# Row-by-row fetches in five steps instead of eight, and two transfers moved to ScalarE's queue, in a graph attention layer

## The chip, the cores and the metric

The kernel runs on one core of a Trainium2 chip. Five engines work in parallel, each in its own fixed order: TensorE (PE, with its weight loads as PEld), VectorE (DVE), ScalarE (ACT), GpSimd (POOL) and SyncE (SP). SyncE, ScalarE and GpSimd can issue transfers, which 16 shared DMA engines carry out. The metric is the device time of one execution in microseconds, as the median over runs; lower is better.

## The reference

One layer of relational graph attention over 3125 nodes with 128 features, 100,000 edges sorted by destination, 5 edge types and 8 heads of 16. Cut to what matters:

```python
for r in range(5):
    q = x[dst] @ W_Q[r];  k = x[src] @ W_K[r];  v = x[src] @ W_V[r]      # per edge, 8 heads
    logits = (q * k).sum(-1) / 4 + attn_bias[r]                          # only edges of type r
    attn = exp(logits - segment_max(logits, dst)) / segment_sum(exp(...), dst)
    out += segment_sum(attn * v, dst)
out = out @ out_proj_w.T + out_proj_b
x = layernorm(x + layernorm(out + x) * ln_gamma + ln_beta)
```

## The kernel before

**Tables first.** A prologue (25 blocks of 128 nodes) computes for each node and each of the 5 types the key and value row (256 numbers of 4 bytes, 1 KB) and writes them to a table `kv_d` in memory; the queries go to `q_d`. From the lists of sources, destinations and types it also makes the row numbers `idx` for gathering, the keys `key_d` (which row of a window of queries an edge needs) and the masks `msk_d` (where a new destination begins).

**Then a loop over edges.** The edges are cut into tiles of 128, four tiles to a group of 512, and three groups to a step: 66 steps (`NST`), the first and the last with two groups. The rows of a tile come into a ring of four places (`place(k)`: three in `kv_early`, one in `kv_late`). In step `k` VectorE multiplies the gathered keys with the queries (`products`, L975), sums them by head (`logits`, L1033) and sets them apart by type (`closed_lanes`); TensorE turns them; two scans of VectorE (L1115, L1119) find the running maximum, which need the masks `mk`; ScalarE takes the exponentials (`exps`, L1137); TensorE turns them back; VectorE weighs the values (`weigh`, L1160), and TensorE sums them by destination (`sums`, L1194) against a matrix that ScalarE makes (`places`, L1173, L1177). Two steps later the sums are divided (`norm`) and put in place (`by_node`), and blocks of nodes that are complete go through the output projection and the two norms.

**Where a tile's rows come from.** Three ways:
- GpSimd gathers most tiles from `kv_d`, one indirect transfer a tile (L849). `point(k, j, leave)` says, at eleven points of a step, up to which tile GpSimd has gathered by then, and after which instruction (`leave`).
- The first tile of each step from 3 to 65 isn't gathered from the table: GpSimd gathers its rows of `x` in the prologue (`xg`, L377), and in the loop ScalarE and TensorE make keys and values of them (`early_places`, `early_turn`, `early_rows`); ScalarE copies them to their place (`early_keep`, L1109).
- In every eighth step (`PERIOD`) one tile is fetched by SyncE, row by row: `own_fetch(k)` loads 16 row numbers into registers (L869) and issues 16 transfers of 1 KB (L875) in each of eight steps; then ScalarE copies the tile to its place (`own_copy`, L883).

**What else is fetched.** `take(k, leave)` runs once a step behind the products and issues on SyncE: the masks of step `k + 2` (`fetch_masks`, L936), the keys of step `k + 3` (`fetch_keys`, L719), and three windows of query rows for step `k + 3` (`fetch_rows`, L743, with a load of three numbers, L704). `own_fetch(k)` follows in the same queue.

**Where the ring's places join.** A step's products cover the tiles from its second one to the first one of the next step, and that one lies at the start of the next place. Between places in `kv_early` that is one stretch. In two of four steps it is two pieces of memory, and `runs` makes two instructions of each product and each sum.

Of the kernel before, what the change touches and what calls it, by code (L numbers as in the profile page):

```python
# [9 lines left out]
F32 = mybir.dt.float32  # L10
BF16 = mybir.dt.bfloat16
# [8 lines left out]
P = 128  # L20
# [3 lines left out]
R = 5  # L24
# [32 lines left out]
WINB = 3 * H * 2  # L57
NTILE = -(-E // P)
LANES = R * HEADS
L3 = G3 * LANES  # L60
SEG = 64
QWB = 10
# [87 lines left out]
def windowed_path(  # L150
# [20 lines left out]
    q_d = dram.tile([NP * R * 3, H], BF16, name="q_d")  # L171
    key_d = dram.tile([NGR, GE], BF16, name="key_d")
    msk_d = dram.tile([NGR, MW], BF16, name="msk_d")


    def keep(name, shape, dt=F32):
        return const.tile(shape, dt, name=name)
# [7 lines left out]
    rows_at = keep("rows_at", [HG, 2, P], I32)  # L185
    oT = keep("oT", [P, N + WN])
    out_wT = keep("out_wT", [P, H])
    gamma_t = keep("gamma_t", [P, H])
# [7 lines left out]

    def kv_tile(name, n):
        pool = ctx.enter_context(tc.tile_pool(name=f"pool_{name}", bufs=1))
        return pool.tile([P, n * T * G3, KVW], F32, name=name)

    early = kv_tile("kv_early", KVA)

# [356 lines left out]
        nc.scalar.copy(typr, typ_r)  # L559

    def own_rows():
        nc.vector.tensor_scalar_mul(rows_at, kvrow[:, :, P : 2 * P], float(KVW * 4))

    msk = load.tile([HG, 2, MW], BF16, name="msk")

# [97 lines left out]
    def late_x():  # L663
# [48 lines left out]

    SPE, ACTE = mybir.EngineType.SP, mybir.EngineType.Activation

    def fetch_keys(k, leave=None):
# [3 lines left out]
        behind(nc.sync.dma_start(kt[:, : n * P], keys.partition_broadcast(P)), leave)  # L719

    def spot(k):
        n = (B0[k + 1] - B0[k]) * P
# [11 lines left out]
        live["hot", k] = hot  # L734
        return made

    def fetch_rows(k, leave=None):
        a, b = G0[k] + (k > 0), min(G0[k + 1] + 1, NGR)
        bytes_ = q_d.rearrange("n h -> (n h)").bitcast(U8)
        for g, f in zip(range(a, b), starts(window, a, b, SPE)):  # L740
            live["qw", g] = qw = ahead.tile([P, 3, H], BF16, name="qw", bufs=QWB)
            behind(
                nc.sync.dma_start(  # L743
                    qw.rearrange("p s h -> p (s h)").bitcast(U8),
                    bytes_[bass.ds(f, P * WINB)].rearrange("(p h) -> p h", h=WINB),
                ),
                leave,
            )

    made = {}  # L750

# [43 lines left out]
    along(keyr, 0, put_key)  # L795
    along(keyr, 1, put_key)
    begins()
    spills()
    types(1, range(R))()
    project_weights()  # L800
# [16 lines left out]
    def place(k):  # L817
        at = k % KVB
        return (early, at * T * G3) if at < KVA else (late, (at - KVA) * T * G3)

    def runs(a, b):
        out_ = []
        for q in range(a, b):
            k = AT[q // T][0]
            kv, at = place(k)
# [31 lines left out]
            issued.append(q)  # L857

    def own_fetch(k):
        at = (k - 2) // PERIOD * PERIOD + PERIOD + 3  # L860
        if at not in OWN_AT:
            return
        i = (k - 2) % PERIOD * ROWS
        if i == 0:
            live["own", at] = flow.tile([P, KVW], F32, name="own")
        n = min(ROWS, P - i)
        g = OWN_AT[at] // T
        bytes_ = kv_d.rearrange("n h -> (n h)").bitcast(U8)
        _, rows = nc.values_load_multi_w_load_instructions(  # L869
            rows_at[g % HG : g % HG + 1, g // HG, i : i + n], engines=[SPE], min_val=0,  # L870
            max_val=(N * R - 1) * KVW * 4,
            skip_runtime_bounds_check_because="sources are nodes, types are relations",
        )
        for p, f in enumerate(rows, i):
            nc.sync.dma_start(  # L875
                live["own", at][p : p + 1].bitcast(U8).rearrange("o (a b) -> o a b", a=2),
                bytes_[bass.ds(f, KVW * 4)].rearrange("(o a b) -> o a b", o=1, a=2),
            )
# [49 lines left out]
        live.pop(("xT", b))  # L928
        store_rows(b, live.pop(("q3", b)))

    def fetch_masks(k, leave=None):
        n = len(groups(k))
        live["mk", k] = mk = flow.tile([L3, MW], BF16, name="mk", bufs=3)
        rows = msk_d[G0[k] : G0[k] + n]
        behind(
            nc.sync.dma_start(  # L936
                mk[: n * LANES, :],
                bass.AP(tensor=rows.tensor, offset=rows.offset, ap=[[MW, n], [0, LANES], [1, MW]]),
            ),
            leave,  # L940
        )

    def spread_q(k):
# [161 lines left out]
            )  # L1105

    def early_keep(k):
        ((kv, c0, _),) = runs(B0[k + 1] - 1, B0[k + 1])
        nc.scalar.copy(kv[:, c0, :], live.pop("rows"))  # L1109

    def scans(k):
        n = len(groups(k)) * LANES
# [293 lines left out]
    spot(1)  # L1406
    fetch_keys(2)
    fetch_rows(2)

    def take(k, leave):  # L1410
# [12 lines left out]
    for k in range(NST - 1):  # L1423
        new, old = k >= 1, k >= 2
        q0, (q, c0, c1), (q1, d0, _) = q_at.get(k), half(k), half(k - 1)
        done, rooted = block_at.get(k), block_at.get(k - 1)
        place_g, sum_g = list(groups(k - 1)), list(groups(k - 1))

        def place_next():
            return places(place_g.pop(0)) if place_g else None  # L1430

        def sum_next():
            if sum_g:
                sums(sum_g.pop(0))
# [681 lines left out]
```

## Time and profile before

| | us |
|---|---|
| median of 3 runs (1009.69 to 1012.93) | 1010.77 |
| the profiled execution, as timed | 1009.02 |
| its span from the first to the last instruction | 1007.2 |
| busy: PE 926.2, DVE 899.2, POOL 741.2, ACT 716.3 | |
| mean granted TensorE clock | 0.979 |

A busy time counts what an engine executes; for SyncE nothing is counted, since issuing a transfer is no busy time, and its timeline is read instead (marked SPq). A row of the timeline gives the start, the length, engine and line, and in brackets the idle time before it with what ended that. A row of a group gives the count, then for one line the shortest, median and longest duration in ns, or busy time and mean ns, and then the idle time before. A row of waits gives the total, the count and the longest. For a transfer the row's length is that of its issue, not of the moving of data.

### The profile page before, as it was taken

How to read it: one execution, taken by the hardware profiler on the slowest of the kernel's cores; microseconds unless marked ns; L12 is line 12 of the kernel's file. 1: busy time of each engine (PE TensorE's matmuls, PEld its weight loads, DVE VectorE, ACT ScalarE, POOL GpSimd, SP SyncE). 2: the span in 40 equal slices, each digit the busy share in tenths (PEclk: the TensorE clock that was granted, in tenths of full speed). 3: DMA queues.
4: the chain of work that ended last, by engine and by line, in shares of the span. 5: the costliest groups of instructions: out<-in, count | busy, mean ns of one | idle time of the engine just before them, and what ended most of it. 6: DMA issues, size and time to landing. Idle time of an engine off the chain costs nothing.

```text
span 1007.2 us, 23071 instructions
## 1 busy us (share of the span) xinstructions
PE 926.2 (92%) x6983; PEld 717.2 (71%) x6983; DVE 899.2 (89%) x1517; ACT 716.3 (71%) x1956; POOL 741.2 (74%) x793
## 2 busy tenths in 40 slices
PE   7995689999999999999999999999999999999986
PEld 3553577777777777777777777778777777777774
DVE  3666788999999999999999999999999999899997
ACT  2443377777787787778777777778777777777765
POOL 7777777777777777777777777777777777777760
PEclk9996799999999999999999999999999999999998
DMA  8997766567666666666666667665666765666630
GB/s 210 356 355 252 206 159 194 158 198 194 177 194 182 179 175 194 177 195 195 177 167 193 195 177 194 178 191 171 193 177 193 194 191 161 185 195 176 160 100 11
DMA packets 100547, 189.60 MB, mean 188 GB/s; under 512 B 19901, under 2 KB 61201, under 8 KB 100298
## 3 DMA queue, kind: packets, MB, share of 16 engines
q0 software_dynamic: 36192, 97.50, 34.9%
q1 hardware_dynamic: 63032, 89.66, 29.7%
q10 hardware_dynamic: 1194, 0.92, 0.4%
q8 instruction: 56, 0.92, 0.4%
q14 instruction: 73, 0.60, 0.2%
HBM read 157.61 MB, written 30.40 MB: 187 GB/s over the span
## 4 chain that ended last, share of the span: by engine, by line
DVE 39%; PE 24%; DMA 21%; issue 8%; POOL 4%; ACT 3%; DVEq 0%; POOLq 0%; ACTq 0%
DMA kv_early<-kv_d,idx 16%; DVE qe L1033 7%; DVE kv_early L975 6%; PE both L1194 5%; PE pr L514 4%; DVE wv L1160 4%; DVE run L1115 4%; DVE run L1119 3%; POOL kv_early L849 3%; PE qe L953 3%; DVE kv_late L975 2%; PE mid L1102 2%; DVE lx L1008 2%; DMA kv_late<-kv_d,idx 2%; PE lt L1092 2%
## 5 line engine op out<-in xcount | busy, mean ns | idle before, releaser
L849 POOL DMA_INDIRECT kv_early<-kv_d,idx x543 | 515.4, 949 | 166.6 <-issue 85.1
L1194 PE MATMUL both<-wv,at 128*125 128x136 f32 x1528 | 261.6, 296 | 0.0
L1173 ACT ACTIVATE at<-wide_at,nkey 128x125 f32<-128x125 f32 x776 | 245.0, 388 | 0.0
L1194 PEld LDWEIGHTS both<-wv,at 128*125 128x125 f32 x1528 | 201.8, 187 | 49.9 <-issue 44.4
L849 POOL DMA_INDIRECT kv_late<-kv_d,idx x169 | 160.0, 947 | 51.5 <-issue 27.1
L1102 PE MATMUL mid<-wkv,xr 128*128 128x256 f32 x630 | 146.5, 379 | 1.6 <-ACT xr L1096 1.6
L953 PE MATMUL qe<-qw,hot 128*128 128x128 bf16 x2349 | 146.1, 222 | 0.0
L953 PEld LDWEIGHTS <-hot 128*128 128x128 bf16 x2352 | 141.6, 102 | 0.5 <-DVE vio L650 0.4
L1102 PEld LDWEIGHTS mid<-wkv,xr 128*128 128x128 f32 x630 | 115.0, 190 | 15.0 <-ACT xr L1096 1.9
L1177 ACT ACTIVATE at<-at 128x500 f32<-128x500 f32 x194 | 120.3, 620 | 6.1
L975 DVE TENSOR_TENSOR kv_early<-kv_early,qe 128x1536 f32<-128x1536 f32 (+3 forms) x70 | 89.3, 1277 | 27.2 <-DMA kv_early<-kv_d,idx 22.0
L1115 DVE TENSOR_TENSOR_SCAN run<-mk,lt 120x640 f32<-120x640 bf16 (+1 forms) x66 | 97.6, 1478 | 1.5 <-PE lt L1065 1.5
L1259 ACT COPY oT<-fin 128x25 f32 x188 | 33.9, 180 | 81.9 <-PE fin L1255 77.9
L1119 DVE TENSOR_TENSOR_SCAN run<-lt,run 120x576 f32<-120x576 bf16 (+1 forms) x65 | 88.2, 1357 | 2.2
L1033 DVE TENSOR_REDUCE qe<-kv_early 128x96 f32<-128x1536 f32 (+2 forms) x65 | 86.7, 1334 | 2.2
L1160 DVE TENSOR_TENSOR wv<-kv_early,mid 128x1536 f32<-128x1536 f32 (+2 forms) x51 | 86.1, 1691 | 1.8 <-PE mid L1102 1.5
L1092 PE MATMUL lt<-diag,xg 128*128 128x512 f32 x252 | 83.5, 454 | 0.0
L1065 PE MATMUL lt<-ident,lx 128*120 128x128 f32 (+2 forms) x396 | 54.7, 275 | 24.6 <-DVE lx L1008 8.6
L1065 PEld LDWEIGHTS lt<-ident,lx 128*120 128x120 f32 (+2 forms) x396 | 38.5, 136 | 52.7 <-ACT diag L1086 20.2
L1144 PEld LDWEIGHTS mid<-gather_heads,ls 120*128 120x128 f32 (+1 forms) x528 | 64.2, 191 | 16.1 <-ACT xTq L901 12.1
L1144 PE MATMUL mid<-gather_heads,ls 120*128 120x24 f32 (+1 forms) x528 | 67.0, 265 | 9.4 <-ACT xTq L901 7.2
L1189 PE MATMUL both<-wv,over 128*5 128x136 f32 x380 | 75.3, 280 | 0.0
(232 smaller groups left out, 1341.5 us busy)
## 6 DMA issues: line engine op xcount, KB each, us to landing
kt<-key_d SPq DMA_DIRECT2D x64, 384.0 KB
qw<-q_d SPq DMA_DIRECT2D x196, 96.0 KB
kv_d<-kvs SPq DMA_DIRECT2D x24, 640.0 KB
own<-kv_d SPq DMA_DIRECT2D x896, 1.0 KB
q_d<-q SPq DMA_DIRECT2D x25, 480.0 KB
mk<-msk_d SPq DMA_DIRECT2D x64, 150.5 KB
kv_early<-kv_d,idx POOLq DMA_INDIRECT x543
kv_late<-kv_d,idx POOLq DMA_INDIRECT x169
```

The costliest lines, as they stand in the source:

```text
L849: nc.gpsimd.indirect_dma_start(out=kv[:, at, :], out_offset=None, in_=kv_d[:, :], in_offset=bass.IndirectOffsetOnAxis(ap=idx[:, q % T, q / ...
L953: spread = nc.tensor.matmul(dest[j], hot[:, j * P : (j + 1) * P], qw[:, c, :], start=(c == 0), stop=(c == 2),)
L975: made = nc.vector.tensor_tensor(kv[:, c0:c1, :H], kv[:, c0:c1, :H], qe[:, n:m], op=ALU.mult)
L1033: made = nc.vector.tensor_reduce(lg[:, n : n + c1 - c0], heads(kv[:, c0:c1, :H]), AX.X, ALU.add)
L1102: nc.tensor.matmul(rows, xr[:, r * P : (r + 1) * P], wkv[:, r].rearrange("h s c -> h (s c)"), start=(r == 0), stop=(r == R - 1),)
L1115: there = nc.vector.tensor_tensor_scan(run[:n], mk[:n, 1 : WIDE + 1], lt, -BIG, op0=ALU.add, op1=ALU.max)
L1119: back = nc.vector.tensor_tensor_scan(run[:n, SEG:][:, ::-1], masks[:, SEG:][:, ::-1], run[:n, SEG:][:, ::-1], -BIG, op0=ALU.add, op1=ALU.max,
L1144: nc.tensor.matmul(ex.rearrange("p (i t) k -> p t i k", t=T)[:, t], ls[: n * LANES, t * P : (t + 1) * P], gather_heads[: n * LANES, :n], s ...
L1160: return nc.vector.tensor_tensor(heads(wv[:, a:b, :H]), heads(kv[:, at + a : at + b, H:]), ex[:, a:b, :, None].to_broadcast([P, b - a, HEA ...
L1173: nc.scalar.activation(at[:, t, :], row_at[:, :WR], AF.Abs, bias=nkey[:, t, g : g + 1], scale=1.0)
L1177: return nc.scalar.activation(at[:, :n], at[:, :n], AF.Relu, bias=1.0, scale=-1.0)
L1194: nc.tensor.matmul(pp[:WR], at[:, t, :], wv[:, T * i + t, :], start=(t == 0), stop=(t == end))
```

## The change

- `PERIOD` becomes 5: 12 tiles instead of 7 are fetched row by row, 26 rows a step instead of 16. Their row numbers go to memory in the prologue (`row_d`) and from there, together with the windows' row numbers, into a table with one row for each step (`at_step`). One load (`load_step`) then fetches both kinds, four steps ahead, in the middle of the rows of the step.
- Masks and keys are issued by ScalarE, behind the second scan and ahead of the exponentials (`ahead_of_both`), and no longer wait for the products. `take` keeps the query rows alone.
- In step 1 the masks from step 6 on are copied five times over in memory (`many_d`); from step 6 a step's masks are read from 15 rows, 8 times each, instead of 3 rows, 40 times each.
- Each place of the ring gets one column more. The first tile of the next step lies there or at the start of the next place, whichever follows without a break; for that `early_keep` copies its keys and its values apart where the places don't join. Products and sums are then one instruction in these steps.

```diff
-PERIOD = 8
+PERIOD = 5
+COPIES = 5
+COPIED = 6
...
-        return pool.tile([P, n * T * G3, KVW], F32, name=name)
+        return pool.tile([P, n * T * G3 + 1, KVW], F32, name=name)
...
-        11: [keys_b],
-        12: [sorted_rows],
-        13: [masks_a],
+        11: [keys_b, own_steps(0)],
+        12: [sorted_rows, own_steps(1)],
+        13: [masks_a, own_steps(2), own_steps(3)],
...
+    def load_step(k):
+        if not 3 <= k < NST - 1:
+            return
+        own = own_part(k - 3)
+        n = own[2] if own else 0
+        _, at = nc.values_load_multi_w_load_instructions(
+            at_step[k : k + 1, : G3 + n], engines=[SPE], min_val=0,
...
+    def beyond(k):
+        kv, at = place(k)
+        return kv, at + T * G3
...
-            at += q - T * G0[k]
+            if q == T * G0[k] and k - 1 in early_at:
+                kv, at = beyond(k - 1)
+            else:
+                kv, at = place(k)
+                at += q - T * G0[k]
...
         for p, f in enumerate(rows, i):
+            if p == i + n // 2:
+                load_step(k + 4)
             nc.sync.dma_start(
...
-    def fetch_masks(k, leave=None):
+    def fetch_masks(k, queue=nc.sync):
...
+        c = COPIES if k >= COPIED else 1
+        rows = (many_d if c > 1 else msk_d)[G0[k] : G0[k] + n]
+        queue.dma_start(
+            mk[: n * LANES, :],
+            bass.AP(
+                tensor=rows.tensor, offset=rows.offset,
+                ap=[[MW, n * c], [0, LANES // c], [1, MW]],
             ),
...
     def early_keep(k):
-        ((kv, c0, _),) = runs(B0[k + 1] - 1, B0[k + 1])
-        nc.scalar.copy(kv[:, c0, :], live.pop("rows"))
+        rows, (kv, c0), (to, c1) = live.pop("rows"), beyond(k), place(k + 1)
+        if kv is to and c0 == c1:
+            nc.scalar.copy(kv[:, c0, :], rows)
+        else:
+            nc.scalar.copy(kv[:, c0, :H], rows[:, :H])
+            nc.scalar.copy(to[:, c1, H:], rows[:, H:])
...
     def take(k, leave):
+        if k + 3 < NST:
+            fetch_rows(k + 3, leave)
+
+    def ahead_of_both(k):
         if k + 2 < NST:
-            fetch_masks(k + 2, leave)
+            fetch_masks(k + 2, nc.scalar)
         if k + 3 < NST:
-            fetch_keys(k + 3, leave)
-            fetch_rows(k + 3, leave)
+            fetch_keys(k + 3, nc.scalar)
...
             take(k, made)
-            if k >= 2:
-                own_fetch(k)
+            own_fetch(k)
+            if k == 1:
+                copy_masks()
...
         for j, leave in enumerate(scans(k)):
             point(k, 2 + j, leave)
+        ahead_of_both(k)
```

More of the change, by code (lines that the diff above doesn't have):

```diff
@@ L173, in windowed_path @@
     msk_d = dram.tile([NGR, MW], BF16, name="msk_d")
+    many_d = dram.tile([NGR, COPIES, MW], BF16, name="many_d")
+    row_d = dram.tile([HG * 2 * P + P], I32, name="row_d")
     def keep(name, shape, dt=F32):
@@ L184, in windowed_path @@
     window = keep("window", [1, NGR], I32)
-    rows_at = keep("rows_at", [HG, 2, P], I32)
+    at_step = keep("at_step", [NST, G3 + ROWS], I32)
     oT = keep("oT", [P, N + WN])
@@ L561, in own_rows, with own_steps, run, window_steps @@
     def own_rows():
-        nc.vector.tensor_scalar_mul(rows_at, kvrow[:, :, P : 2 * P], float(KVW * 4))
+        rows_at = srt.rearrange("g s i -> g (s i)").bitcast(I32)[:, : 2 * P]
+        nc.vector.tensor_scalar_mul(
+            rows_at.rearrange("g (s i) -> g s i", s=2), kvrow[:, :, P : 2 * P], float(KVW * 4)
+        )
+        nc.sync.dma_start(
+            row_d[: HG * 2 * P].rearrange("(g i) -> g i", g=HG), rows_at
+        )
+    def own_steps(i):
+        def run():
+            for k in list(OWN_AT)[i::4]:
+                g = OWN_AT[k] // T
+                a, f = (g % HG * 2 + g // HG) * P, k - PERIOD - 1 + 3
+                nc.sync.dma_start(
+                    at_step[f : f + PERIOD, G3:],
+                    row_d[a : a + PERIOD * ROWS].rearrange("(i j) -> i j", j=ROWS),
+                )
+        return run
+    def window_steps():
+        nc.sync.dma_start(
+            at_step[3 : NST - 1, :G3],
+            window[:, G0[3] + 1 : G0[NST - 1] + 1].rearrange("o (k j) -> o k j", j=G3),
+        )
     msk = load.tile([HG, 2, MW], BF16, name="msk")
@@ L713, in windowed_path, with fetch_keys @@
     SPE, ACTE = mybir.EngineType.SP, mybir.EngineType.Activation
-    def fetch_keys(k, leave=None):
+    def fetch_keys(k, queue=nc.sync):
         n = B0[k + 1] - B0[k]
@@ L718, in fetch_keys @@
         keys = key_d.rearrange("g e -> (g e)")[B0[k] * P : B0[k + 1] * P]
-        behind(nc.sync.dma_start(kt[:, : n * P], keys.partition_broadcast(P)), leave)
+        queue.dma_start(kt[:, : n * P], keys.partition_broadcast(P))
     def spot(k):
@@ L735, in spot @@
         return made
+    def load_step(k):
[5 more added lines that the diff above has]
+            at_step[k : k + 1, : G3 + n], engines=[SPE], min_val=0,
+            max_val=(N * R - 1) * KVW * 4,
+            skip_runtime_bounds_check_because="rows of nodes, sources and types",
+        )
+        live["at_step", k] = [
+            nc.s_assert_within(
+                f, 0, (N - 1) * R * WINB,
+                skip_runtime_bounds_check_because="destinations are nodes",
+            )
+            for f in at[:G3]
+        ] + list(at[G3:])
     def fetch_rows(k, leave=None):
@@ L739, in fetch_rows @@
         bytes_ = q_d.rearrange("n h -> (n h)").bitcast(U8)
-        for g, f in zip(range(a, b), starts(window, a, b, SPE)):
+        if 3 <= k < NST - 1:
+            at = live.pop(("at_step", k))
+            live["rows_at", k - 3] = at[G3:]
+        else:
+            at = starts(window, a, b, SPE)
+        for g, f in zip(range(a, b), at):
             live["qw", g] = qw = ahead.tile([P, 3, H], BF16, name="qw", bufs=QWB)
@@ L748, in fetch_rows, with own_part @@
             )
+    def own_part(k):
+        at = (k - 2) // PERIOD * PERIOD + PERIOD + 3
+        if k < 2 or at not in OWN_AT:
+            return None
+        i = (k - 2) % PERIOD * ROWS
+        return at, i, min(ROWS, P - i)
     made = {}
@@ L797, in windowed_path @@
     begins()
+    window_steps()
     spills()
@@ L824, in runs @@
             k = AT[q // T][0]
-            kv, at = place(k)
-            at += q - T * G0[k]
+            if q == T * G0[k] and k - 1 in early_at:
[3 more added lines that the diff above has]
+                at += q - T * G0[k]
             if out_ and out_[-1][0] is kv and out_[-1][2] == at:
@@ L859, in own_fetch @@
     def own_fetch(k):
-        at = (k - 2) // PERIOD * PERIOD + PERIOD + 3
-        if at not in OWN_AT:
+        rows = live.pop(("rows_at", k), None)
+        if not rows:
+            load_step(k + 4)
             return
-        i = (k - 2) % PERIOD * ROWS
+        at, i, n = own_part(k)
         if i == 0:
             live["own", at] = flow.tile([P, KVW], F32, name="own")
-        n = min(ROWS, P - i)
-        g = OWN_AT[at] // T
         bytes_ = kv_d.rearrange("n h -> (n h)").bitcast(U8)
[L869 to L873, printed above, removed]
         for p, f in enumerate(rows, i):
+            if p == i + n // 2:
+                load_step(k + 4)
             nc.sync.dma_start(
@@ L929, in store_q, with copy_masks @@
         store_rows(b, live.pop(("q3", b)))
-    def fetch_masks(k, leave=None):
+    def fetch_masks(k, queue=nc.sync):
         n = len(groups(k))
         live["mk", k] = mk = flow.tile([L3, MW], BF16, name="mk", bufs=3)
[L934 to L938, printed above, removed]
-            ),
-            leave,
+        c = COPIES if k >= COPIED else 1
[5 more added lines that the diff above has]
+                ap=[[MW, n * c], [0, LANES // c], [1, MW]],
+            ),
+        )
+    def copy_masks():
+        nc.sync.dma_start(
+            many_d[G0[COPIED] :],
+            msk_d[G0[COPIED] :, None, :].to_broadcast([NGR - G0[COPIED], COPIES, MW]),
         )
@@ L1107, in early_keep @@
     def early_keep(k):
-        ((kv, c0, _),) = runs(B0[k + 1] - 1, B0[k + 1])
-        nc.scalar.copy(kv[:, c0, :], live.pop("rows"))
+        rows, (kv, c0), (to, c1) = live.pop("rows"), beyond(k), place(k + 1)
+        if kv is to and c0 == c1:
+            nc.scalar.copy(kv[:, c0, :], rows)
+        else:
+            nc.scalar.copy(kv[:, c0, :H], rows[:, :H])
+            nc.scalar.copy(to[:, c1, H:], rows[:, H:])
     def scans(k):
@@ L1408, in windowed_path @@
     fetch_rows(2)
+    load_step(3)
     def take(k, leave):
+        if k + 3 < NST:
+            fetch_rows(k + 3, leave)
+    def ahead_of_both(k):
         if k + 2 < NST:
-            fetch_masks(k + 2, leave)
+            fetch_masks(k + 2, nc.scalar)
         if k + 3 < NST:
-            fetch_keys(k + 3, leave)
-            fetch_rows(k + 3, leave)
+            fetch_keys(k + 3, nc.scalar)
     def half(k):
```

## The prediction

> **What bounds the kernel now.** I read the busy shares first, then the stretches, then each engine's waits, and only then the chain. In one stretch of 600 us from the middle (columns: length, then PE, PEld, DVE, ACT and POOL busy, granted clock, share of the DMA engines, GB/s), below the page's span, TensorE and VectorE look like the bound:
>
> ```profile
> span 1007.2 us, 23071 instructions
> 200.00:800.00 600.00, 571.71 (x4555) 455.95 (x4554) 567.94 (x898) 463.66 (x1268) 454.00 (x480) 1.00 0.66 185
> ```
>
> The stretch has 571.71 us of TensorE and 454.00 of GpSimd in 600. But GpSimd's records leave out a gap of its own after each gather. The timeline of GpSimd, first gathers, two from the middle and the last ones, and its longest waits:
>
> ```profile
> 3.99 1.10 POOL L377 DMA_INDIRECT xg<-in_x,xf  x1 [1.35 <-DMA xf<-in_src]
> ...
> 500.02 0.95 POOL L849 DMA_INDIRECT kv_early<-kv_d,idx  x1 [0.30 <-issue]
> 501.27 0.95 POOL L849 DMA_INDIRECT kv_early<-kv_d,idx  x1 [0.31 <-issue]
> ...
> 976.99 0.94 POOL L849 DMA_INDIRECT kv_early<-kv_d,idx  x1 [0.30 <-issue]
> ```
>
> ```profile
> L377 POOL DMA_INDIRECT xg<-in_x,xf x3: 945/947/1102, 4.0 to 6.6; - x3
> L377 POOL DMA_INDIRECT xg<-in_x,xi x60: 940/944/2239, 7.9 to 83.5; - x60
> L849 POOL DMA_INDIRECT kv_early<-kv_d,idx x543: 942/946/1380, 84.7 to 977.0; - x181
> L849 POOL DMA_INDIRECT kv_late<-kv_d,idx x169: 942/946/1064, 125.4 to 956.0; - x169
> POOL kv_early L849 <- issue: 85.1, 279, 0.3
> POOL kv_early L849 <- DVE kv_early L975: 5.9, 16, 1.3
> ```
>
> There are 3 + 60 + 543 + 169 = 775 gathers; the first starts at 3.99 and the last at 976.99, so one takes (976.99 - 3.99) / 774 = 1.257 us, and between two in the middle lie 501.27 - 500.02 = 1.25. The gap is 0.3 whatever precedes it; in the last row the longest is 1.3, once, near the end. So from 4 us to 977 the time is a count of gathers, and 1007.2 - 977.9 = 29.3 us of tail follow. A step of the loop (3 groups, 12 tiles, one of them made from x, so 11 gathers) takes 11 x 1.25 = 13.75, less one gather in eight steps: 13.75 - 1.25 / 8 = 13.59 us. TensorE uses 571.71 / 600 x 13.59 = 12.95 of it, VectorE (567.94) 12.86, ScalarE (463.66) 10.50.
>
> **The change part by part.** *Fewer gathers.* SyncE now fetches a whole tile row by row in 5 steps instead of 8: tiles for steps 11, 19, ... 59 (7) become tiles for steps 8, 13, ... 63 (12). GpSimd loses 5 gathers: 5 x 1.25 = 6.25 us, directly on the bound. The new mean step is 13.75 - 1.25 / 5 = 13.50. All else must fit under that.
>
> *SyncE's step.* Its timeline over two steps, with two looks at one row each and one at three consecutive rows, the register load, and its waits in the same 600 us:
>
> ```profile
> 497.87 0.74 SPq L936 DMA_DIRECT2D mk<-msk_d  x1
> 498.66 0.48 SPq L719 DMA_DIRECT2D kt<-key_d  x1
> 500.24 1.35 SPq L743 DMA_DIRECT2D qw<-q_d  x3
> 502.72 8.38 SPq L875 DMA_DIRECT2D own<-kv_d  x16
> 504.91 0.23 SPq L875 DMA_DIRECT2D own<-kv_d  x1
> 506.06 0.23 SPq L875 DMA_DIRECT2D own<-kv_d  x1
> 512.55 0.45 SPq L719 DMA_DIRECT2D kt<-key_d  x1
> 516.68 6.45 SPq L875 DMA_DIRECT2D own<-kv_d  x16
> 518.67 0.23 SPq L875 DMA_DIRECT2D own<-kv_d  x1
> 521.93 0.87 SPq L875 DMA_DIRECT2D own<-kv_d  x3
> 524.17 0.37 SPq L1376 DMA_DIRECT2D out<-z  x1
> L869 SPq TENSOR_LOAD <-rows_at x56: 974/1020/1212, 135.1 to 883.1; - x56
> SPq L875 <- DMA kt<-key_d: 34.3, 40, 1.5
> SPq L875 <- DMA qw<-q_d: 24.5, 67, 1.1
> SPq L875 <- DMA mk<-msk_d: 13.2, 23, 1.4
> SPq L875 <- DMA own<-kv_d: 1.7, 7, 0.3
> ```
>
> Three rows take 0.87, so one follows the next after (0.87 - 0.23) / 2 = 0.32. Now: 16 x 0.32 = 5.1, masks 0.74, keys 0.45, query rows 1.35, two loads 2 x 1.02, one store 0.37: 10.1 us, and waits of (34.3 + 24.5 + 13.2 + 1.7) / 44 steps = 1.7. After: 26 x 0.32 = 8.3, query rows 1.35, one load 1.0 (`load_step` fetches windows and rows together, four steps ahead), a store 0.4: 11.1 us. With the same 1.7 of waits that is 12.8 against 13.50. It fits by 0.7; with the waits of the first step shown (8.38 - 15 x 0.32 - 0.23 = 3.35) it would not (14.4), with those of the second (6.45 - 5.03 = 1.4) it would (12.5). I take 1.7, since masks and keys, to which (34.3 + 13.2) of the 73.7 us are put down, leave this queue.
>
> *ScalarE's step.* It now issues masks and keys, 0.74 + 0.48 = 1.2 us, between the second scan and the exponentials. What it has there:
>
> ```profile
> L1137 ACT ACTIVATE ls<-ls 120x512 f32<-120x512 f32 x64 | 40.4, 632 | 32.4 <-DVE ls L1129 32.2
> L1109 ACT COPY kv_early<-mid 128x256 f32<-128x256 f32 x47 | 16.6, 353 | 0.0
> L392 ACT COPY xT<-tp 128x128 f32<-128x128 f32 x24 | 6.6, 277 | 7.9 <-PE tp L390 4.1 <-PE pr L514 3.7
> ```
>
> The exponentials already wait 32.2 us for VectorE in 64 steps, 0.5 each; that covers part of the 1.2, the rest delays them by 0.7. In half the steps the kept tile is copied as two halves: 2 x 0.277 - 0.353 = 0.2, so 0.1 a step; 5 more copies of fetched tiles, priced by the same row, are 5 x 0.353 = 2 us in all. ScalarE goes to 10.50 + 1.2 + 0.1 = 11.8 of 13.50. I take it as hidden behind the 1.7 us that are left; a gain is excluded, since it is work added.
>
> *VectorE, keys uncut.* Where a step's tiles lay in two places, product and reduction were cut in two:
>
> ```profile
> L1033 DVE TENSOR_REDUCE qe<-kv_early 128x96 f32<-128x1536 f32 x31 | 54.6, 1761 | 1.1
> L975 DVE TENSOR_TENSOR kv_early<-kv_early,qe 128x1536 f32<-128x1536 f32 x31 | 54.4, 1753 | 16.9 <-DMA kv_early<-kv_d,idx 14.6 <-ACT xTq L901 1.2 <-issue 1.0
> L1033 DVE TENSOR_REDUCE qe<-kv_late 128x88 f32<-128x1408 f32 x16 | 26.0, 1627 | 0.6
> L975 DVE TENSOR_TENSOR kv_early<-kv_early,qe 128x1408 f32<-128x1408 f32 x16 | 25.9, 1621 | 10.3 <-DMA kv_early<-kv_d,idx 7.4 <-DMA kv_late<-kv_d,idx 2.7
> L1033 DVE TENSOR_REDUCE qe<-kv_late 128x8 f32<-128x128 f32 x16 | 4.7, 295 | 0.6
> L975 DVE TENSOR_TENSOR kv_late<-kv_late,qe 128x128 f32<-128x128 f32 x16 | 4.5, 280 | 0.0
> ```
>
> A cut step saves 1.621 + 0.280 - 1.753 = 0.15 and 1.627 + 0.295 - 1.761 = 0.16, in half the steps: 12.86 - 0.15 = 12.7 of 13.50. It gives VectorE room and moves the end by nothing; the cover is GpSimd, and without it it would be 32 x 0.31 = 10 us.
>
> *Masks five times over.* A copy of (196 - 17) x 5 x 1284 bytes = 1.15 MB in step 1; at the 185 GB/s of the stretch 6 us, two steps ahead of its first reader. From step 6 the 120 reads come from 15 rows instead of 3. In the first step shown the row at 504.91 starts as the masks of 497.87 land, 7.0 us later, and the row at 506.06 as the keys of 498.66 do, after 7.4, though the keys are 128 x 1536 elements and the masks 120 x 642. The Trainium skill (DMA: Bandwidth & Descriptors, "Why a DMA increments its semaphore by 16 and not by 1") says that a transfer runs on the largest number of engines, up to 16, that divides the slowest dimension of both sides: 3 for 3 x 40 rows, 15 for 15 x 8. The trace agrees with it so far as a transfer 2.5 times smaller lands in the same time; by that rule the masks would land sooner and keys and rows would no longer queue behind them on three engines, and SyncE's 1.7 us would shrink. The sum keeps 1.7 us.
>
> *Prologue.* Fourteen small transfers more on SyncE, at 0.23 to 0.5 us some 5 us, against this wait of its own in 30 to 84 us, so nothing:
>
> ```profile
> SPq L524 <- DVE kvs L517: 24.8, 14, 3.8
> ```
>
> *Sum.* -6.25 + 0 + 0 + 0. The profiled execution took 1009.02, so 1002.8 by its scale; it lies 1.75 under the median of 1010.77, and against the median I forecast **1004.5**.
>
> **The rivals.** *Slower: one ring of semaphores for two queues.* Rows wait for landings that they have no data from, and early in the kernel SyncE does so for a load that ScalarE issued:
>
> ```profile
> SPq L263 <- DMA wn<-in_L_gnn_W_K: 1.2, 2, 0.9
> wn<-in_L_gnn_W_K ACTq DMA_DIRECT2D x1, 256.0 KB
> ```
>
> So transfers of both queues take turns on the same few semaphores (eight, as I read the records), and each waits until its predecessor there has landed. Before, everything was in one queue and in order. After, a row of SyncE can wait for keys that ScalarE has yet to issue, and ScalarE's masks for a row that SyncE has yet to issue; behind ScalarE's wait stand the exponentials, TensorE's turn of them and all later places. The loop: keys land (from 512.55 to the held row at 518.67, 6.1; 7.4 in the step before), 14 rows x 0.32 = 4.5, the load 1.0, the landing of a row (under 8 x 0.32 = 2.6, as rows hardly wait for rows), and the next keys. That is 14.2 to 15.5 us; it decides from 13.5. I take 14.4, near the lower end, as the masks ahead of the keys are spread: 60 steps x 0.9 = 54 over the forecast: 1058. For it: SyncE's 73.7 us of such waits. Against it: 0.9 us off a landing, and the loop is no longer than the step; and which row stands before which transfer on a semaphore is not in the profile. The Trainium skill (DMA: Bandwidth & Descriptors, "Bandwidth") tells to batch transfers to a MiB or more, and 26 rows of 1 KB go against that. No run here shows what that costs beside the 0.32 of a row in the queue.
>
> *Slower: ScalarE's 0.7 us is not hidden.* If the three compute engines are already abreast of GpSimd (13.59), less 0.15 for VectorE, plus 0.82: 14.26, 62 steps x 0.67 = 42: 1052. For it ScalarE's order is fixed, so that all behind the exponentials is late; against it, its 1.7 us of idle time left.
>
> *No change.* GpSimd is relieved and TensorE takes over: if 571.71 of 600 is as full as it gets, a step stays at 12.95 / 0.953 = 13.59: 1010.8. Against it the waits for gathers before L975 above, 14.6 us, which say that the data is waited for.
>
> **How the numbers follow.** Forecast 0.50, ring 0.26, ScalarE 0.10, no change 0.14. A measurement tells about 0.3%, 3 us. Faster 0.52 (the forecast, and a little of the no-change case), same 0.13, slower 0.35. The likeliest case alone is 1001 to 1008. The range has to reach the slower cases: up to 1058 it leaves out half the ring case and some of the rest.
>
> **What would show it.** Right: 770 gathers 1.25 apart without longer gaps, the last starting near 970.7; rows 26 a step, done before the next products; masks landing sooner. Ring: gaps over 0.3 on GpSimd, the exponentials late, SyncE's and ScalarE's waits named by each other's transfers. Wrong altogether: GpSimd waiting on VectorE in every step without such waits.

## The result, and the profile after

The changed kernel takes 1377.73 us (median; 1374.12 to 1387.96) where the kernel before took 1011.02 beside it: ratio 1.364, 95% interval 1.359 to 1.369. Forecast were 1004.5 us, with a range up to 1058. The profiled execution took 1374.12 us. The ratios here and below are taken from undisturbed runs alone, so one can differ a little from that of the two medians.

The page of the changed kernel: span, busy shares, the chain's shares by engine, and the group of most gathers:

```profile
span 1372.3 us, 24266 instructions
...
PE 984.2 (72%) x6983; PEld 764.8 (56%) x6983; DVE 899.2 (66%) x1453; ACT 720.7 (53%) x1993; POOL 735.1 (54%) x788
...
PE 44%; SPq 19%; DVE 11%; DMA 10%; issue 7%; ACT 5%; ACTq 3%; POOL 1%; DVEq 0%; POOLq 0%
...
L914 POOL DMA_INDIRECT kv_early<-kv_d,idx x534 | 506.1, 948 | 461.0 <-ACT at L1249 142.8
```

Of the busy times only TensorE's has grown by much (984.2 us against 926.2, at a mean granted clock of 0.853 against 0.979); every other engine is idle for a third of the span or more. A gather still takes 0.948 us, but GpSimd now sits idle for 461 us before this group, where it was 166.6, first of all for ScalarE. The chain has SyncE's queue at 19%. So the question for the waits (engine, line, what was waited for: us in total, times, longest) is who holds ScalarE:

```profile
ACT kv_early L944 <- DMA own<-kv_d: 184.5, 8, 24.2
ACT kv_late L944 <- DMA own<-kv_d: 67.0, 3, 23.9
ACT ls L1209 <- DMA mk<-msk_d: 53.4, 2, 52.1
ACT kv_early L944 <- DMA out<-z: 23.4, 1, 23.4
...
SPq L936 <- DMA mk<-many_d: 174.3, 35, 9.3
SPq L936 <- DMA kt<-key_d: 97.3, 52, 3.7
```

L944 is `own_copy`, the copy of the tile that SyncE fetched row by row (L936). All 12 copies wait, 184.5 + 67.0 + 23.4 = 274.9 us, 22.9 each. And one wait of 52.1 stands before the exponentials, once, early. SyncE's rows, on their side, wait 271.6 us for masks and keys, which carry no data for them.

The timeline of one such meeting, first ScalarE's queue, then SyncE's, each row a transfer with its start and the time it took to issue:

```profile
520.32 1.34 ACTq L997 DMA_DIRECT2D mk<-many_d  x1
521.76 0.74 ACTq L746 DMA_DIRECT2D kt<-key_d  x1
...
535.21 1.34 ACTq L997 DMA_DIRECT2D mk<-many_d  x1
536.59 0.33 ACTq L746 DMA_DIRECT2D kt<-key_d  x1
```

```profile
516.79 0.57 SPq L936 DMA_DIRECT2D own<-kv_d  x2
524.23 0.23 SPq L936 DMA_DIRECT2D own<-kv_d  x1
525.89 0.23 SPq L936 DMA_DIRECT2D own<-kv_d  x1
...
538.32 0.23 SPq L936 DMA_DIRECT2D own<-kv_d  x1
541.16 0.23 SPq L936 DMA_DIRECT2D own<-kv_d  x1
```

Two rows go out at 516.79 and 517.13; the next goes out at 524.23. ScalarE issued its masks only at 520.32, three microseconds *after* SyncE had come to that row, and they landed at 524.2. In the records of these instructions the row of 524.23 and the masks of 520.32 name the same semaphore (104), and so do 525.89 and the keys of 521.76 (106), 538.32 and the masks of 535.21 (108), 541.16 and the keys of 536.59 (101). Each of the four rows goes out 0.02 us after the transfer ahead of it on its semaphore has landed (524.21, 525.87, 538.30 and 541.14).

The records show the same over the whole loop: behind 116 of the masks and keys that ScalarE issues, 58 of each, the next transfer on the semaphore is a row of SyncE, and their order is not that of the steps. A row's number tells its step (26 rows a step, 128 a tile): 24 of these rows belong to the step in which ScalarE issues the masks or keys, 48 to the step before it, 42 to two steps before, 2 to the step after. The row of 524.23 is one of step 18 and waits for masks issued in step 20. So SyncE cannot get ahead of ScalarE, and in most steps it is made to trail it. Such a row is called tied below.

What that costs shows where ScalarE needs the tile:

```profile
547.80 0.27 ACT L1181 COPY kv_early<-mid 128x128 f32<-128x128 f32 x1
571.97 0.40 ACT L944 COPY kv_late<-own 128x256 f32<-128x256 f32 x1 [23.90 <-DMA own<-kv_d]
```

```profile
545.09 11.48 SPq L936 DMA_DIRECT2D own<-kv_d  x26
...
559.42 1.35 SPq L793 DMA_DIRECT2D qw<-q_d  x3
560.88 10.03 SPq L936 DMA_DIRECT2D own<-kv_d  x24
```

```profile
552.75 0.95 POOL L914 DMA_INDIRECT kv_early<-kv_d,idx  x1 [0.30 <-issue]
576.67 0.94 POOL L914 DMA_INDIRECT kv_early<-kv_d,idx  x1 [22.97 <-ACT at L1249]
```

ScalarE comes to the copy at 548.07. SyncE is a step and three quarters behind: it has most of 26 rows and a whole further part of 24 to issue, and ends at 570.9. The length of the stall follows from the order of the semaphores: the row of 541.16 is number 72 of the 128 of its tile, counted from 0, and the last one that is tied to ScalarE in this way; 55 rows follow it. In the ten tiles from the second to the eleventh the last row goes out 29.6 us (median) after the last tied one, and ScalarE comes to the copy 7.4 us after it. ScalarE's order is fixed, so the exponentials, TensorE and all places stand behind the copy, and GpSimd's gathers stop for 23 us. Counted from one exponentials to the next, four steps of 12 to 18 us and one of 34 to 38 are the pattern of the whole loop.

### The profile page after: what moved, and what is told of

The parts are those of the page before. It is cut to its first block, busy times and chain, and to the rows that moved or that the text cites. A ratio compares the mean times of both kernels' runs of the same rounds, so it can differ in the third digit from the quotient of the medians.

```text
span 1372.3 us, 24266 instructions
## 1 busy us (share of the span) xinstructions
PE 984.2 (72%) x6983; PEld 764.8 (56%) x6983; DVE 899.2 (66%) x1453; ACT 720.7 (53%) x1993; POOL 735.1 (54%) x788
## 3 DMA queue, kind: packets, MB, share of 16 engines
q1 hardware_dynamic: 48599, 57.16, 12.9%
## 4 chain that ended last, share of the span: by engine, by line
PE 44%; SPq 19%; DVE 11%; DMA 10%; issue 7%; ACT 5%; ACTq 3%; POOL 1%; DVEq 0%; POOLq 0%
SPq L936 11%; PE both L1266 8%; PE mid L1170 8%; PE qe L1021 6%; PE lt L1160 6%; PE mid L1216 5%; SPq L793 5%; SPq L769 4%; PE pr L518 3%; DMA qw<-q_d 3%; PE both L1261 2%; PE fin L1327 2%; ACTq L997 2%; ACT ls L1209 2%; PE lt L1133 2%
## 5 line engine op out<-in xcount | busy, mean ns | idle before, releaser
L1216 PE MATMUL mid<-gather_heads,ls 120*128 120x24 f32 (+1 forms) x528 | 81.1, 294 | 320.0 <-ACT ls L1209 225.2
L1266 PE MATMUL both<-wv,at 128*125 128x136 f32 x1528 | 277.8, 309 | 0.9 <-ACT at L1249 0.7
L1216 PEld LDWEIGHTS mid<-gather_heads,ls 120*128 120x128 f32 (+1 forms) x528 | 74.5, 218 | 333.3 <-ACT ls L1209 233.4
L1266 PEld LDWEIGHTS both<-wv,at 128*125 128x125 f32 x1528 | 217.3, 200 | 54.1 <-issue 47.5
L1021 PE MATMUL qe<-qw,hot 128*128 128x128 bf16 x2349 | 157.9, 229 | 27.5 <-DMA qw<-q_d 26.9
L1170 PE MATMUL mid<-wkv,xr 128*128 128x256 f32 x630 | 147.2, 381 | 1.6 <-ACT xr L1164 1.6
L1043 DVE TENSOR_TENSOR kv_early<-kv_early,qe 128x1536 f32<-128x1536 f32 (+4 forms) x54 | 86.7, 1606 | 61.1 <-ACT kv_early L944 60.6
L1170 PEld LDWEIGHTS mid<-wkv,xr 128*128 128x128 f32 x630 | 115.8, 192 | 15.1 <-ACT xr L1164 1.9
L977 DVE TENSOR_TENSOR fin<-fin,q 128x384 f32<-128x384 f32 (+1 forms) x42 | 20.4, 485 | 157.4 <-ACT q L973 157.4
L1209 ACT ACTIVATE ls<-ls 120x512 f32<-120x512 f32 (+1 forms) x66 | 41.6, 630 | 140.8 <-DMA mk<-msk_d 53.4
L944 ACT COPY kv_early<-own 128x256 f32<-128x256 f32 x9 | 3.6, 404 | 207.9 <-DMA own<-kv_d 184.5
L1160 PE MATMUL lt<-diag,xg 128*128 128x512 f32 x252 | 99.8, 526 | 0.0
L756 DVE TENSOR_SCALAR hot<-kt,row_of 128x512 bf16<-128x512 bf16 x196 | 61.7, 370 | 26.8 <-PE qe L1021 18.8
```

Of the source, the lines that this page charges most:

```text
L1021: spread = nc.tensor.matmul(dest[j], hot[:, j * P : (j + 1) * P], qw[:, c, :], start=(c == 0), stop=(c == 2),)
L1043: made = nc.vector.tensor_tensor(kv[:, c0:c1, :H], kv[:, c0:c1, :H], qe[:, n:m], op=ALU.mult)
L1160: nc.tensor.matmul(lt[:, c0:c1], xg[:, e, :], at[:, c0:c1], start=True, stop=True)
L1170: nc.tensor.matmul(rows, xr[:, r * P : (r + 1) * P], wkv[:, r].rearrange("h s c -> h (s c)"), start=(r == 0), stop=(r == R - 1),)
L1216: nc.tensor.matmul(ex.rearrange("p (i t) k -> p t i k", t=T)[:, t], ls[: n * LANES, t * P : (t + 1) * P], gather_heads[: n * LANES, :n], s ...
L1266: nc.tensor.matmul(pp[:WR], at[:, t, :], wv[:, T * i + t, :], start=(t == 0), stop=(t == end))
```

## Experiments

Times are medians beside runs of the kernel before on the same chip; each ratio is to these.

### Who is to blame: the queue, the rows or ScalarE

**e1_one_queue**: masks and keys back on SyncE, all else as changed.

```diff
-            fetch_masks(k + 2, nc.scalar)
+            fetch_masks(k + 2)
-            fetch_keys(k + 3, nc.scalar)
+            fetch_keys(k + 3)
```

> The changed kernel with masks and keys issued by SyncE again, at the place behind the second scan; five steps, spread masks and uncut keys stay. Theory (rows of SyncE stand on shared semaphores behind masks and keys that ScalarE issues only a step or two later): the eleven stalls of some 24 us at the copy of the fetched tile go, ScalarE's wait there is under 10 us in sum, and SyncE has 11.1 + 1.2 + 1.7 = 14.0 us a step at worst: 1003 to 1040 us. Rival 'SyncE is too slow for 26 rows a step': it gets 1.2 us more to do, so the time stays over 1370, toward 1378 + 60 x 1.2 = 1450. Rival 'ScalarE's own issue time and order': 1003 to 1011, which this run alone does not tell from the theory.

Measured: 1227.34 us, ratio 1.217 (1.214 to 1.219). The waits at the copy are gone, but the time is 187 us over the 1040 that the theory allowed at most. Neither theory alone holds.

**e2_eight_steps**: `PERIOD = 8` in the changed kernel.

> The changed kernel with one tile in eight steps instead of five, 16 rows a step; ScalarE still issues masks and keys. Theory of the shared semaphores: the stalls stay, one for each of 7 tiles instead of 12, about 25 us each: 1011 + 7 x 25 = 1186, and somewhere in 1100 to 1250 us; the wait at the copy of the fetched tile remains ScalarE's longest. Rival 'SyncE is too slow for 26 rows': 16 rows fitted before, so 1005 to 1015. Rival 'ScalarE's issue': as with five steps, 1360 to 1380.

Measured: 1137.33 us, ratio 1.127 (1.124 to 1.129). The stalls stay with 16 rows a step, one in eight steps, but smaller (62.4 us in 7, below), and the wait of 50 us early on stays as well. In the records the last tied row of a tile is now number 98 of 128; the last row goes out 15.5 us after it, and ScalarE comes to the copy 6.9 us after it (medians); the difference, 8.6, and the landing of the last row make the stalls of mostly 9 to 11 us.

**e3_no_rows**: `OWN_AT = {}`, no tile fetched by SyncE.

> The changed kernel without any tile fetched by SyncE: GpSimd gathers those 12 tiles too (782 gathers); ScalarE still issues masks and keys, masks are spread, keys uncut. Theory of the shared semaphores and rival 'SyncE is too slow' both say: nothing is late any more, 7 gathers more than the kernel before, 1011 + 7 x 1.25 = 1020 us (1015 to 1030). Rival 'ScalarE's issue and order': the loss of 367 us stays, over 1300 us. If masks and keys themselves come late by SyncE's query rows, the result lies between.

Measured: 1054.43 us, ratio 1.045 (1.043 to 1.047). Without rows nearly all of the loss goes; what stays over the count of gathers is about 35 us, and its wait list shows one wait of 37.6 for `mk<-msk_d` where the changed kernel had 52.1. So a third cause acts once, early, with no row involved.

**e4_two_later**: each fetched tile is used two steps later.

```diff
-OWN_AT = {k: T * G0[k] + T + 1 for k in range(PERIOD + 3, NST - 2, PERIOD)}
+OWN_AT = {k: T * G0[k] + T + 1 for k in range(PERIOD + 5, NST - 2, PERIOD)}
-        at = (k - 2) // PERIOD * PERIOD + PERIOD + 3
+        at = (k - 2) // PERIOD * PERIOD + PERIOD + 5
```

> The changed kernel with each fetched tile used two steps later than now (tiles for steps 10, 15, ... 60, eleven of them, 771 gathers), so the copy has two steps, some 28 us, more until it needs the rows. Theory of the shared semaphores: SyncE is held back by a bounded lag, that of the transfers it waits for, and the waits of 24 us at the copy measure it; 28 us more hide nearly all of it: 1004 to 1070 us. Rival 'SyncE is too slow for 26 rows': what it lacks in every step adds up whatever the head start: over 1340 us. Rival 'ScalarE's issue': unchanged, about 1378.

Measured: 1261.51 us, ratio 1.249 (1.246 to 1.252). Wrong for the theory as I had put it: the waits at the copy go, but the time stays far over the 1070 that it allowed at most. The order on the semaphores has moved with the edit (93 of 101 tied rows now stand behind masks or keys of two steps later), and the query rows that SyncE also issues are late; that is where the waits are now:

```profile
PE qe L1021 <- DMA qw<-q_d: 125.0, 50, 7.8
POOL kv_early L914 <- PE qe L1021: 115.9, 29, 9.6
```

### The third cause: a copy of 179 rows

Around the early wait stands the copy of the masks. SyncE's timeline in the changed kernel:

```profile
124.23 0.72 SPq L1006 DMA_DIRECT2D many_d<-msk_d  x1
132.21 52.04 SPq L793 DMA_DIRECT2D qw<-q_d  x3
184.37 16.25 SPq L936 DMA_DIRECT2D own<-kv_d  x26
```

The copy's last landing stands 66.3 us after its issue in the trace, and the three query rows behind it, elsewhere 1.35 us, take 52.04 to issue. ScalarE's wait hangs on this by a shared semaphore as well: its masks of 191.80 come next on number 107 behind SyncE's row of 185.21, which landed at 191.8. The prediction gave the copy 6 us, from the rate of all transfers together. The Trainium skill (DMA: Bandwidth & Descriptors, "Why a DMA increments its semaphore by 16 and not by 1") has the rule that I used for the reads and not for the copy: the largest number up to 16 that divides both slowest dimensions. For 179, a prime, that is 1 engine, for 176 it is 16. The trace agrees as far as it shows: the semaphore of the copy gets two increments, one at its issue and one at the end, and that of 176 rows in f3 below gets 16; the copy's 895 rows in 66.3 us are 74 ns each.

**e5_copy_cut** and, on other chips, **e9_copy_cut_2** and **f3_copy_cut_3**: the changed kernel with the copy in two parts.

```diff
-        nc.sync.dma_start(
-            many_d[G0[COPIED] :],
-            msk_d[G0[COPIED] :, None, :].to_broadcast([NGR - G0[COPIED], COPIES, MW]),
-        )
+        part = (NGR - G0[COPIED]) // 16 * 16
+        for a, b in ((G0[COPIED], G0[COPIED] + part), (G0[COPIED] + part, NGR)):
+            nc.sync.dma_start(
+                many_d[a:b], msk_d[a:b, None, :].to_broadcast([b - a, COPIES, MW])
+            )
```

> The changed kernel with the copy of the masks cut in two transfers, 176 rows and 3 rows, instead of one of 179; nothing else. Theory: 179 is a prime, so the one transfer runs on a single engine (it landed 66 us after its issue, and SyncE's next transfer, a query row, took 52 us to issue); 176 rows go to 16 engines and land within 10 us, SyncE is free again, and the stall of 52 us before the exponentials of the third step goes: 1378 - 45 = 1333 (1320 to 1345). Rival 'that stall is the first meeting of the two queues on the semaphores': it stays, 1365 to 1385.

> The kernel of e5_copy_cut again, since the chip of the last four runs took 1338 us for the kernel before, with TensorE's products slower. There the two parts of the copy landed after 11.3 and 10.3 us instead of 66, and the stalls of 24 us every five steps stayed although its other steps took 18 us, in which SyncE has room. On a chip where the kernel before takes 1011: theory, the stall of 52 us goes and the others stay, 1378 - 45 = 1333 (1320 to 1345). Rival 'the 52 us only move to another wait': 1365 to 1385.

> The kernel of e5_copy_cut once more (the change with the copy cut in two, nothing else). Where the kernel before takes 1011, theory: 1378 - 45 = 1333 (1320 to 1345). Rival 'the 52 us only move to another wait': 1365 to 1385.

Measured: 1597.05 us beside 1338.01 for the kernel before (ratio 1.193, 1.185 to 1.201), 1568.04 beside 1314.96 (1.191, 1.183 to 1.198), and 1332.23 beside 1012.49 (1.314, 1.311 to 1.317). The first two were run on chips that are slower with the kernel before as well (last section), so only their ratios count. The third answers the question: 1333 was expected, 1332 came. The parts land 10.6 and 10.1 us after issue, and SyncE goes on:

```profile
123.94 1.43 SPq L1008 DMA_DIRECT2D many_d<-msk_d  x2
137.34 1.33 SPq L793 DMA_DIRECT2D qw<-q_d  x3
138.80 5.46 SPq L936 DMA_DIRECT2D own<-kv_d  x11
```

So the copy cost 1377.7 - 1332.2 = 45.5 us; e1 against f1 below gives 45.2, and e3 against f2, without rows, 30.0. The slower chips say something more. There a step between two stalls takes 17 to 18 us on average, in which SyncE would have room (it needs some 15, an estimate from f1's rows below without masks and keys), and yet the copies of the fetched tile wait as long. What ended ScalarE's idle time at L944 in f3_copy_cut_3, then in e9_copy_cut_2 (us, times):

```profile
  DMA own<-kv_d: 274.2, 12
```

```profile
  DMA own<-kv_d: 268.9, 12
```

22.9 and 22.4 us each. A queue that was only too slow would have caught up there; a queue tied to ScalarE's transfers cannot.

### One edit at a time, with the copy cut

**f1_five_one_queue_cut** is e1 with the copy cut; **f2_no_rows_cut** is e3 with it.

> e1_one_queue with the copy cut in two: five steps, 26 rows, masks and keys issued by SyncE. SyncE's step there, from its rows in e1: 26 x 0.324 + 2.2 (load) + 1.5 (query rows) + 1.6 (masks, keys) + 0.4 (stores) = 14.1, and 1.75 of waits: 15.9 to 16.1 us. Theory, SyncE's rate is its bound and nothing else: 1227 - 45 = 1180 (1165 to 1190), steps of 16. Rival 'what was slow in e1 was the aftermath of the copy': 1005 to 1020.

Measured: 1182.11 us, ratio 1.168 (1.165 to 1.171), 2 us from the expected. SyncE's timeline over one step, its load of rows, and what waits for it:

```profile
513.07 0.88 SPq L997 DMA_DIRECT2D mk<-many_d  x1
514.01 0.54 SPq L746 DMA_DIRECT2D kt<-key_d  x1
514.74 1.32 SPq L793 DMA_DIRECT2D qw<-q_d  x3
516.18 13.21 SPq L936 DMA_DIRECT2D own<-kv_d  x26
529.48 0.38 SPq L719 DMA_DIRECT2D q_d<-q  x1
529.91 0.90 SPq L997 DMA_DIRECT2D mk<-many_d  x1
```

```profile
L769 SPq TENSOR_LOAD <-at_step x62: 680/2192/2455, 109.1 to 1096.9; - x62
...
DVE hot L756 <- DMA kt<-key_d: 141.9, 47, 6.6
...
SPq L936 <- DMA kt<-key_d: 49.8, 54, 2.1
```

From masks to masks SyncE takes 16.8 us; 13.21 of it are 26 rows with the load among them, and that load of up to 29 values takes 2.19 us where the one of 16 took 1.02. VectorE waits for keys that SyncE issues too late. In this form 26 rows a step are simply too many.

> e3_no_rows with the copy cut in two: no tile fetched by SyncE, 782 gathers; ScalarE issues masks and keys. Theory: the 35 us that e3 had over the count of its gathers were the copy: 1011 + 7 x 1.25 = 1020 (1010 to 1022). Rival 'they were ScalarE's issue, 0.6 us a step': 1050 as before.

Measured: 1024.40 us, ratio 1.012 (1.010 to 1.014). Seven gathers more are 8.8 us of the 11.9; at most 3 us are left for ScalarE's issue, which is longer than priced:

```profile
L997 ACTq DMA_DIRECT2D mk<-many_d x60: 1279/1344/1374, 171.9 to 978.7; - x60
```

So 26 rows with all on one queue (f1) cost 169 us over f4 below, ScalarE's issue without rows (f2) next to nothing, and rows with ScalarE's issue (f3) 319, though there SyncE has less to issue than in f1. What is added is their meeting.

**e6_eight_one_queue_cut**, repeated as **e10_eight_one_queue_cut_2** and **f4_eight_one_queue_cut_3**, has eight steps, the copy cut, and SyncE issuing; **e8_eight_cut** and **e11_eight_cut_2** differ from it only in that ScalarE issues; **e7_eight_later_cut** is e8 with the tile used two steps later.

> The changed kernel with the copy cut in two, one tile in eight steps and masks and keys issued by SyncE: what is left of the change is the spread masks, the uncut keys and the load of rows four steps ahead. Theory: of the 367 us the copy, SyncE's rate and the shared semaphores are the whole, so 1003 to 1013 us, no wait for a fetched tile over 1 us. Rival 'spread masks or uncut keys cost time themselves': 1020 or more.

> The changed kernel with the copy cut in two, one tile in eight steps, each used two steps later than now; ScalarE issues masks and keys. With 16 rows SyncE has room (the steps between the stalls took 13.6 to 13.9), so what is late there is late by the shared semaphores alone. Theory: the lag is bounded (11 us at each copy with eight steps) and two steps, 27 us, more hide it: 1137 - 45 - 77 = 1015 (1008 to 1030). Rival 'ScalarE's issue delays the step': the head start brings nothing, 1080 to 1095, as the same kernel without it.

> The changed kernel with the copy cut in two and one tile in eight steps; ScalarE issues masks and keys. It differs from e6_eight_one_queue_cut in nothing but the engine that issues masks and keys, and from e7_eight_later_cut in nothing but the head start. Theory of the shared semaphores: seven stalls of 11 us stay, 1137 - 45 = 1092 (1080 to 1100), 77 us over e6. Rival 'the stalls come from the long copy early on': without it they go, 1005 to 1020.

> The kernel of e6_eight_one_queue_cut again (ratio 1.002 where the kernel before took 1338). On a chip where it takes 1011 and GpSimd, not TensorE, is the bound: theory, 1003 to 1013 us. Rival 'spread masks or uncut keys cost time themselves': 1020 or more.

> The kernel of e8_eight_cut again (ratio 1.035 where the kernel before took 1338). It differs from e10_eight_one_queue_cut_2 only in that ScalarE issues masks and keys. Theory of the shared semaphores, with seven stalls of 11 us: 1137 - 45 = 1092 (1080 to 1100). Rival 'with the copy out of the way the two queues no longer meet': 1005 to 1020.

> The kernel of e6_eight_one_queue_cut once more (ratio 1.002 and 1.000 where the kernel before took 1338 and 1315). Where the kernel before takes 1011 and GpSimd is the bound, theory: 1003 to 1013 us, as spread masks and uncut keys lie beside the bound. Rival 'spread masks or uncut keys cost time': 1020 or more.

| kernel | us | before, same chip | ratio (95%) |
|---|---|---|---|
| e6, SyncE issues | 1340.99 | 1338.01 | 1.002 (0.998 to 1.006) |
| e8, ScalarE issues | 1384.57 | 1338.01 | 1.035 (1.028 to 1.042) |
| e7, ScalarE issues, two steps later | 1352.86 | 1338.01 | 1.010 (1.006 to 1.014) |
| e10, SyncE issues | 1315.30 | 1314.96 | 1.000 (0.995 to 1.004) |
| e11, ScalarE issues | 1354.62 | 1314.96 | 1.021 (1.013 to 1.030) |
| f4, SyncE issues | 1013.41 | 1012.49 | 1.000 (0.998 to 1.002) |

The pairs e6/e8 and e10/e11 are two kernels with one difference, the issuing engine, and 16 rows a step, which fit: by the ratios 3.3% and 2.2% slower with ScalarE. Where the kernel before takes 1011 this pair was not run; an estimate is e2 less the copy, 1137.3 - 45.5 = 1091.8, against f4 with 1013.4: 78 us, or 94 with the copy at 30.0. The copies of the fetched tile waited 62.4 in e2 and not at all in f4. In e7 the head start takes the waits at the copy away and some 70% of the loss with them, as expected for a bounded lag, though the order on the semaphores has moved with it as in e4 (96 of 117 tied rows stand behind masks or keys of two steps later; in e8 73 of 107 behind those of one step later). The expected times of this group were for the faster chips, where only f4 was run. And f4 shows that spread masks, uncut keys and the load ahead, taken together, change nothing that can be measured.

### Whether five gathers fewer bring 6.25 us

**g1_five_left_out** and **g2_three_left_out** take f1 and leave the rows out altogether: 12 tiles, and with `PERIOD = 3` in g2 20 tiles, are neither gathered nor fetched nor copied.

```diff
     def own_part(k):
-        if k < 2 or at not in OWN_AT:
+        if True:
             return None
     def own_copy(k):
-        if k in OWN_AT:
+        if False:
```

> e10_eight_one_queue_cut_2 with one tile in five steps instead of eight, where those 12 tiles are neither gathered by GpSimd nor fetched row by row nor copied (the tile keeps what lay there: that part of the computation is left out). 770 gathers instead of 775. Theory 'GpSimd's count of gathers is the bound': 5 x 1.25 = 6.25 us less than the kernel before, 1004 to 1007 where that takes 1011 to 1012. Rival 'TensorE takes over at the step of 13.6': no difference that can be measured, 1009 to 1013.

> The same with one tile in three steps left out (20 tiles, for steps 6, 9, ... 63; 762 gathers). Theory 'count of gathers': 13 x 1.25 = 16 us less than the kernel before, 995 to 997. Rival 'TensorE takes over': 1008 to 1013.

Measured: 1009.10 us beside 1011.53 (ratio 0.997, 0.996 to 0.999) and 1001.49 (0.990, 0.988 to 0.993): 2.7 us by the ratio for 5 gathers, 9.8 for 13, where the count gives 6.25 and 16. The gathers of g1, with the first and last start:

```profile
L914 POOL DMA_INDIRECT kv_early<-kv_d,idx x534: 940/946/1325, 86.4 to 973.0; - x178
L914 POOL DMA_INDIRECT kv_late<-kv_d,idx x173: 940/946/1089, 127.0 to 951.7; - x173
```

The last starts at 973.0 instead of 977.0, but the span is 1007.2 as before: the tail is 4 us longer in this execution. In g2 the gathers themselves are held: what GpSimd's gaps before them have beyond 0.33 us adds up to 8.1 us, where it was 2.0 before. The gathers are fewer, yet the other engines follow only in part. In the stretch of 200 to 800 us TensorE is busy for 580.80 of 600 in g2 (571.71 before, 578.22 in f4):

```profile
200.00:800.00 600.00, 580.80 (x4641) 465.92 (x4640) 572.10 (x872) 471.32 (x1309) 454.20 (x479) 1.00 0.63 185
```

## Why the prediction was wrong, point by point

- **Rival 1 was the mechanism, with the wrong price: the step that failed.** The prediction named the shared semaphores and asked how long the loop of one step becomes: 14.4 us, 0.9 a step, 54 us; the forecast itself put the meeting of the queues at nothing and kept 1.7 us of waits a step, since masks and keys would leave this queue. In the changed kernel SyncE waits 271.6 us for just these masks and keys, 4.5 in each of 60 steps. The prediction left open which row stands behind which transfer. The records show rows that wait for masks and keys of one or two steps later, so SyncE cannot run ahead of ScalarE and trails it by over a step; and that this is paid not as 0.9 in each step but at one place, `own_copy`, with 22.9 us in every fifth step: 274.9 us. The prediction followed SyncE's lag to the next step's start, and not to the instruction that uses what SyncE fetches. For the price, e8 against e6 (16 rows, one difference) shows the meeting by itself, f3 against f1 and f2 with 26 rows. No run gave the two queues semaphores of their own, so that this alone would end the loss is not shown.
- **SyncE's step of 11.1 us: the load was mis-sized.** `load_step` was put at one load of 1.0, from a row with 16 values; it takes 2.17 to 2.19 for up to 29. With 8.3 + 1.35 + 2.2 + 0.4 = 12.3 and the same 1.7 of waits SyncE needs 14.0 of 13.50, and the room of 0.7 on which the forecast rested was not there. That alone would be an estimated 60 x 0.5 = 30 us; no run has it by itself.
- **The masks' copy: 6 us were 66, and 45.5 on the end.** It was priced by the mean rate of many transfers; this one, as 179 rows in one piece, landed after 66.3 us, and cut in two after 10.6. "Two steps ahead of its first reader" was true and did not help: what was held is SyncE's next transfer, which took 51 us to issue, and what stood behind it, not the reader.
- **5 gathers, 6.25 us: about 2.7.** The bound was read rightly, but g1 and g2 bring less than the count, 2.7 us of 6.25 and 9.8 of 16; that the compute engines are nearly abreast of GpSimd is the likely reason and not shown. The third rival (no change) had more to it than 0.14. By that, even with all else as priced, the forecast would have been some 1008.
- **ScalarE's issue as hidden: right.** 1.34 + 0.33 = 1.7 us instead of 1.2, yet at most 3 us in all by f2, where a step has 13.75 us by its gathers.
- **VectorE, keys uncut: right, beside the bound.** In f4 the product of 63 steps is one of 128 x 1536, with no rest of 128 x 128:

```profile
L1044 DVE TENSOR_TENSOR kv_early<-kv_early,qe 128x1536 f32<-128x1536 f32 x47 | 82.2, 1750 | 20.5 <-DMA kv_early<-kv_d,idx 9.7 <-DMA kv_late<-kv_d,idx 5.7 <-ACT xTq L962 2.8
L1044 DVE TENSOR_TENSOR kv_late<-kv_late,qe 128x1536 f32<-128x1536 f32 x16 | 28.0, 1749 | 3.3 <-DMA kv_late<-kv_d,idx 3.0 <-issue 0.2
```

- **Masks land sooner: right.** From the rows above, 524.23 - 520.32 = 3.9 and 538.32 - 535.21 = 3.1 us instead of 7.0; their issue by SyncE took 0.88 instead of 0.74 us.

No version beat the kernel before by what can be measured, apart from those that leave work out. Whether six or seven steps with one queue would was not tried. From f1's rows, six steps (22 rows x 0.32 + 2.0 for the load + 1.3 + 1.4 + 0.4 and 1.7 of waits) are an estimated 13.8 us, still over the 13.5 of the step; seven (19 rows) are some 12.9, which fit, for one gather fewer.

## What to carry to other kernels

Moving transfers to a second queue may tie the queues together: look in the records which semaphores they share, and follow a lag to the instruction that needs what the late queue brings, for a fixed order turns it into one long stall of all engines. Price each single transfer by its own shape, a large one above all, and ask what is queued behind it. Ask how much the bound is worth before relieving it: here 13 gathers fewer, 16 us by the count, brought 9.8, one per cent. A change that loads a queue to its limit for so little risks much.

## What the runs showed of the hardware

- SyncE's and ScalarE's transfers stood on the same eight semaphores, and a row of SyncE went out 0.02 us after ScalarE's masks ahead of it on its semaphore had landed (524.21 and 524.23).
- A transfer of 179 rows from DRAM to DRAM landed after 66 us, and SyncE's next took 51 to issue; 176 and 3 rows landed after 10.6 and 10.1.
- A register load of up to 29 values took 2.19 us and one of up to 19 took 1.91 (f4), about twice the 1.02 of one with 16 from another table; why it is so much longer was not studied.
- The same masks cost SyncE 0.88 and ScalarE 1.34 us to issue.
- On two of the chips the kernel before took 1338 and 1315 us instead of 1011 to 1012. TensorE's group at L1170/L1171 there and here (e10_eight_one_queue_cut_2, e3_no_rows):

```profile
L1171 PE MATMUL mid<-wkv,xr 128*128 128x256 f32 x630 | 184.4, 450 | 93.5 <-ACT xr L1165 76.6 <-issue 13.0 <-ACT q L982 3.9
```

```profile
L1170 PE MATMUL mid<-wkv,xr 128*128 128x256 f32 x630 | 146.8, 380 | 1.6 <-ACT xr L1164 1.6
```

This group takes 450 against 380 ns, the others of TensorE less more (310 against 299 at L1267/L1266); VectorE's and GpSimd's own durations are the same within a per cent (a gather 0.946 against 0.952). The mean granted clock of the kernel before was about 0.88 on those chips and 0.97 on the others. Why they were slower was not studied.
